# Reordering the tail of the last block: a written order for three engines, a bf16 bias product, and int8 products pulled forward

## The chip, the cores and the metric

The kernel runs on one core of a Trainium2 chip. The core has a matrix engine (TensorE, PE in the profile; its weight loads are PEld), a vector engine (VectorE, DVE), an activation engine (ScalarE, ACT), a general engine (GpSimd, POOL), and a queue engine that issues most transfers (SyncE, SP). The metric is the device time of one execution in microseconds (us); the time of a version is the median of its runs.

## What is computed

Two layers act on `x` of shape (2, 2048, 512). The first is a conditioned linear layer, a gated recurrence over the tokens and a gated MLP. The second, where the change lies, does this for every token:

```python
h = silu(cat @ int_W1 + int_b1) @ int_W2 + int_b2      # cat: six normed or shifted forms of x
y = (h - mean(h)) / sqrt(var(h) + 1e-5) * int_g + int_be
scale = max(abs(y)) / 127                              # per token
q = clip(round(y / scale), -127, 127)                  # int8 values, held as bf16
x = x + (q @ q_rhs) * scale * rhs_scale
```

## The kernel before, in words

One program does both layers. The first phase lasts to about 1392 us and works on 1024 tokens at a time. The second phase works on 8 blocks of 512 tokens (`T`), and a block is four tiles of 128 tokens (`J` = 4).

For a block, `by_tokens` and `by_channels` make the operands of the first product; `up` (its steps are those of `paired_in_place`, all products through line 134) computes the hidden values `h1` in seven steps, with half products that are reused: the steps are numbered 0 to 6, and each has a half `u` = 0 and a half `u` = 1. Helpers hang on the steps in a dictionary `then`: a key `n` runs after step n, a key `(n, u)` after that half. `added` (L1486) adds the class bias with a bf16 product against `tables[:30, 3]`. The sums are finished on VectorE (L1474, L1495, L1500), and SiLU (L1478) runs on ACT. The last half of `h1` for tokens 0 to 255 comes from `out21`, after step 6.

In blocks 0 to 6, `down2` makes the second product `h1 @ int_W2`, and the norm and the int8 part of a block are spread over the next block's steps. The last block has no next block. For it `part_norm` (from L1591) makes one tile's second product and norm, and rounds it; `part_product` (from L1613) turns the rounded values by four TensorE transposes, clamps them at -127, makes the int8 product (L1548, called from `by_rhs`), scales it (L1551), adds the residual (L1620) and stores the tile (L1621). Tiles 2 and 3 get their `part_norm` after `(6, 0)`, since their hidden values are complete then. Tiles 0 and 1 follow after step 6, and then `part_product` of tiles 2, 3, 0, 1.

In `part_norm` the bias `int_b2` is added by a product of a row of ones with the row `b2_bc[0:1]`, both f32 (L1596). An f32 product of 512 columns is two instructions on TensorE, so the four chunks of `int_W2` are eight (L1598). The norm on VectorE is: statistics from PSUM (L1320, L1321), variance plus eps (L1327), root on ACT (L1328), subtract and gain (L1533), reciprocal and a three-instruction refinement (L1329, L86 to L88), scale and shift (L1534), largest magnitude (L1537), the two scale instructions (L1045, L1046), scaling with a rounding constant added (`shifted`, L1540), and the constant taken off with the upper clamp (`rounded`, L1543).

What sets the order: each engine has a queue that it works off in order. The framework's scheduler fills the queues from simulated times and priorities (text order), so it may lift an instruction ahead of others and mix two chains. Inside `tc.manual_schedule(engines=...)` the listed engines take instructions in the order in which they are written; `ordered()` is that for PE, DVE and ACT. The first block already uses it for PE alone. Waits between engines are semaphores; SP and POOL are queues too, and a transfer that waits holds those behind it.

The second phase's small buffers come from the pool `io`, in the order in which `place` first names them: `rows` (bias, gain and shift, broadcast to 128 partitions, loaded at L1301), `int_w2`, then `pw1`, `lnT`, `tT` and so on. They lie over buffers of the first phase: in the kernel before, `pw1` begins 14,336 bytes into the pool. `split` (L1110 to L1114) cuts an f32 row into three bf16 parts whose sum is the row, on POOL, and stores the parts into `tables`; the class bias of the second phase takes this way, around 1414 us. `tables` has 128 partitions and 4 slots of 512 bf16; slot 3 uses rows 0 to 29.

Of the kernel before, what the change touches and what calls it, by code (L numbers as in the profile page):

```python
# [9 lines left out]
FP = mybir.dt.float32  # L10
BF = mybir.dt.bfloat16
AF = mybir.ActivationFunctionType
ALU = mybir.AluOpType
# [4 lines left out]
P = 128  # L18
B, L, D, F = 2, 2048, 512, 1536
C = D // P  # L20
FC = F // P
T = 512
J = T // P
# [6 lines left out]
G = 32  # L30
MAGIC = 12582912.0
# [19 lines left out]
def adaln_attn_ffn(ctx: ExitStack, tc: tile.TileContext, a: dict, out: bass.AP):  # L51
    nc = tc.nc
# [3 lines left out]
    small = ctx.enter_context(tc.tile_pool(name="small", bufs=2))  # L56
# [53 lines left out]
    def mm(name):  # L110
        return mm_ps.tile([P, T], FP, tag="mm", name=name)
# [217 lines left out]
    ones = const.tile([P, P], FP, name="ones")  # L329
# [4 lines left out]
    identb = const.tile([P, P], BF, name="identb")  # L334
# [33 lines left out]
    idle = mm("idle")  # L368
# [185 lines left out]
    def up_norm(s):  # L554
        return normed_halves(2, s, hs_d[s], "L0_attn_norm2_w")
# [297 lines left out]
    for s in range(1, NS):  # L853
        Bt, chunks = up_norm(s)
# [13 lines left out]
    rq = w3.tile([P, C, D], BF, name="rq", bufs=1)  # L868
    rsbc = w3.tile([P, D], FP, name="rsbc", bufs=1)
# [5 lines left out]
    tables = w3.tile([P, 4, D], BF, name="tables", bufs=1)  # L875
# [406 lines left out]
    def place(name, *shape, dtype=FP):  # L1282
        if name not in places:
            n = 1
            for k in shape:
                n *= k
            places[name] = io.tile([P, n], FP if dtype == FP else BF, name=name)
        t = places[name]
        if dtype != FP and t.dtype == FP:
            t = t.bitcast(dtype)  # L1290
        if len(shape) == 2:
            return t.rearrange("p (a b) -> p a b", b=shape[1])
        return t
# [8 lines left out]
    b2_bc, g_bc, be_bc = (rows[:, k, :] for k in range(3))  # L1302
    w2 = place("int_w2", C, D)
    load_w(w2, a["int_W2"])


    PAIRS = (0, 1)

    def duo(t, q):
# [4 lines left out]
    def tr(name, dtype=FP):  # L1314
        turn[0] ^= 1
        return tr_ps[turn[0]].tile([P, 2, D], dtype, tag="tr", name=name)

    def stats(mv, j, t, name):
        st = small.tile([P, 6], FP, tag="st", name=f"{name}_st_{j}", bufs=4)
        nc.vector.bn_stats(st, t)  # L1320
        held["stats"] = nc.vector.bn_aggr(mv[:, j, :], st)  # L1321

    def rstd_of(mv, name):
        n = mv.shape[1]
        r = small.tile([P, J], FP, tag="rstd", name=f"{name}_rstd", bufs=4)[:, :n]
        v = small.tile([P, 2, J], FP, tag="rv", name=f"{name}_rv", bufs=4)[:, :, :n]
        nc.vector.tensor_scalar(v[:, 0, :], mv[:, :, 1], 1e-5, None, ALU.add)  # L1327
        held["root"] = nc.scalar.activation(r, v[:, 0, :], AF.Sqrt)  # L1328
        nc.vector.reciprocal(r, r)  # L1329
        refine(r, v[:, 0, :], v[:, 1, :])  # L1330
        return r
# [36 lines left out]
    def by_tokens(i, k, behind=()):  # L1368
# [6 lines left out]
        mv = small.tile([P, J, 2], FP, tag="mv", name=f"mv1_{i}", bufs=4)  # L1375
        for q in PAIRS:
            if behind:
# [52 lines left out]
    def gains(i, k, n):  # L1430
# [4 lines left out]
        else:  # L1435

            src = block("lnT")
            dst = block("tT") if n == (not i) else src
        ps = [tr(f"gain_{i}_{n}_{q}") for q in PAIRS]
        for c in range(C):  # L1440
# [8 lines left out]
    h1s, o4s, mvs = {}, {}, {}  # L1449
# [81 lines left out]
    def gained(out_, in_, mean, r):  # L1531

        nc.vector.scalar_tensor_tensor(out_, in_, mean, g_bc, ALU.subtract, ALU.mult)  # L1533
        nc.vector.scalar_tensor_tensor(out_, out_, r, be_bc, ALU.mult, ALU.add)  # L1534

    def largest(out_, t):
        nc.vector.tensor_reduce(out_, t, AX.X, ALU.max, apply_absolute_value=True)  # L1537

    def shifted(t, inv):
        nc.vector.tensor_scalar(t, t, inv, MAGIC, ALU.mult, ALU.add)  # L1540

    def rounded(qn, t):
        nc.vector.tensor_scalar(qn, t, -MAGIC, 127.0, ALU.add, ALU.min)  # L1543

    def by_rhs(t, qT, scale, name):
        ps = m2_ps.tile([P, D], FP, tag="mm", name=name)
        for c in range(C):
            nc.tensor.matmul(  # L1548
                ps, qT[:, ts(c, P)], rq[:, c, :], start=(c == 0), stop=(c == C - 1)
            )  # L1550
        nc.vector.scalar_tensor_tensor(t, ps, scale, rsbc, ALU.mult, ALU.mult)  # L1551

    out_t = out.rearrange("(n p) d -> p n d", p=P)
# [34 lines left out]
        nc.vector.tensor_add(t, t, duo(x2n, q))  # L1588
        nc.sync.dma_start(out_t[:, i * J + 2 * q : i * J + 2 * q + 2], t)

    def part_norm(i, j):  # L1591


        h1 = h1s[i]
        ps = m2_ps.tile([P, D], FP, tag="mm", name=f"ps_o_{i}_{j}")
        nc.tensor.matmul(ps, ones[0:1, :], b2_bc[0:1, :], start=True, stop=False)  # L1596
        for c in range(C):
            nc.tensor.matmul(ps, h1[:, c, ts(j, P)], w2[:, c, :], start=False, stop=(c == C - 1))  # L1598
        mv = small.tile([P, J, 2], FP, tag="mv", name=f"mv3_{i}_{j}", bufs=4)[:, 0:1]
        stats(mv, 0, ps, f"s3_{i}_{j}")  # L1600
        r = rstd_of(mv, f"r3_{i}_{j}")
        t = place(f"o4_{j // 2}", 2, D)[:, j % 2, :]
        gained(t, ps, mv[:, 0, 0:1], r[:, 0:1])
        qs = small.tile([P, 3, J], FP, tag="qs4", name=f"qs_{i}_{j}", bufs=4)[:, :, 0:1]
        largest(qs[:, 0, :], t)
        quant_scale(qs[:, 1, :], qs[:, 2, :], qs[:, 0, :])
        shifted(t, qs[:, 2, :])

        qn = places["pw0"].bitcast(BF)[:, ts(j, D)]
        rounded(qn, t)  # L1610
        return t, qs, qn

    def part_product(i, j, t, qs, qn):  # L1613
        pt = tr(f"trq_{i}_{j}", BF)[:, 0, :]
        for c in range(C):
            nc.tensor.transpose(pt[:, ts(c, P)], qn[:, ts(c, P)], identb)
        qT = places["pw1"].bitcast(BF)[:, ts(j, D)]
        nc.vector.tensor_scalar(qT, pt, -127.0, None, ALU.max)
        by_rhs(t, qT, qs[:, 1, :], f"ps_f_{i}_{j}")
        nc.vector.tensor_add(t, t, place(f"x2n{i % 2}", J, D)[:, j, :])  # L1620
        nc.sync.dma_start(out_t[:, i * J + j], t)  # L1621

# [18 lines left out]
    for m, at in ((0, 0), (2, 2)):  # L1641
        for c in range(C):
            nc.tensor.matmul(
                pb[G * c : G * c + G], beta(m, c), w_int[at + c // 2][:, 1:4:2, c % 2, :],
                start=(m == 0), stop=(m == 2),
            )
    for c in range(C):
        nc.tensor.matmul(
            pc[G * c : G * c + G], beta(1, c), w_int[2 + c // 2][:, 0:3:2, c % 2, :],
            start=True, stop=True,  # L1650
# [40 lines left out]
    for i in range(NB):  # L1691
        nxt = load(i + 1) if i + 1 < NB else None
        then = {} if last else in_first
        if last:
            qs = []
            then[0] = lambda: qs.append(last_norm(i - 1))
            then[1] = lambda: [int8_values(i - 1, qs[0], q) for q in PAIRS]
            then[2] = lambda: int8_product(i - 1, qs[0], last["x2n"], 0, held["ins"])
            then[3, 0] = lambda: int8_product(i - 1, qs[0], last["x2n"], 1, held["ins"])
        if nxt:  # L1700
            then[3] = lambda: by_tokens(i + 1, nxt)
            then[6] = lambda: by_channels(i + 1, nxt)
        else:

            parts = {}

            def half():
                for j in (2, 3):
                    parts[j] = part_norm(i, j)
            then[6, 0] = half  # L1710
        up(i, k, then)
        if nxt:
            down2(i, nxt)
        else:
            for j in (0, 1):
                parts[j] = part_norm(i, j)
            for j in (2, 3, 0, 1):
                part_product(i, j, *parts[j])
        last, k = k, nxt


# [66 lines left out]
```

## Time and profile before

| what | value |
|---|---|
| median of 3 runs | 2020.08 us (2018.74 to 2021.53) |
| the profiled execution, its own time | 2021.65 us |
| its span | 2019.9 us |
| TensorE busy | 2001.7 us, 99% of the span |
| VectorE busy | 1174.8 us, 58% |
| ACT busy | 653.4 us, 32% |
| POOL busy | 153.8 us, 8% |

The span runs from the first to the last instruction; the execution's own time is a little longer. Busy time of an engine is the time in which it runs an instruction; a wait is not counted. "The chain that ended last" goes back from the last instruction to what released it. In the order of time, a row holds the start, the duration, the engine, the line, the operation, what is written and read, and the count of merged instructions; in square brackets stands the idle time before it and what ended it. In a row of windows, after the window and its length come the busy time and the count of PE, PEld, DVE, ACT and POOL, then the granted TensorE clock (1.00 is full), the transfer engines' busy share, and GB/s.

### The profile page before, as it was taken

The numbers are of one execution on the slowest core, as the hardware profiler recorded it, in microseconds if no ns is written. First come the engines' busy times: TensorE is split into PE (matmuls) and PEld (weight loads), VectorE is DVE, ScalarE is ACT, GpSimd is POOL, SyncE is SP. The second block draws the span as 40 slices with busy tenths as digits, with TensorE's granted clock in tenths as the row PEclk, the third lists the DMA queues.
The fourth block names the chain that finished last, engine by engine and source line by source line (L and its number), as shares of the span: only waits on it lengthen the run. The fifth ranks groups of instructions, "written<-read, shape, count | busy, mean of one in ns | idle before, by whom it ended". The sixth has DMA issues, their size and how long they took to land.

```text
span 2019.9 us, 16905 instructions
## 1 busy us (share of the span) xinstructions
PE 2001.7 (99%) x6292; PEld 1067.4 (53%) x6300; DVE 1174.8 (58%) x1783; ACT 653.4 (32%) x863; POOL 153.8 (8%) x127
## 2 busy tenths in 40 slices
PE   9999999999999999999999999989999999999998
PEld 5444444444444444444444444435877777777774
DVE  6667666666534224324325465466687687687675
ACT  4557777777522222222221000001302302302301
POOL 0141000000400000000010000061300000000000
PEclk9999999999999999999999999999999999999999
DMA  5661212121512112111335766533211211211110
GB/s 202 217 198 52 90 62 98 42 94 58 161 42 91 45 42 94 42 42 52 110 112 180 229 220 224 201 111 130 92 45 63 76 51 63 73 53 63 32 32 21
DMA packets 99332, 197.21 MB, mean 98 GB/s; under 512 B 21393, under 2 KB 49591, under 8 KB 95153
## 3 DMA queue, kind: packets, MB, share of 16 engines
q1 hardware_dynamic: 94584, 179.31, 26.4%
q0 software_dynamic: 4608, 16.78, 2.5%
q8 instruction: 50, 0.82, 0.2%
q14 instruction: 34, 0.27, 0.0%
q10 hardware_dynamic: 56, 0.03, 0.0%
HBM read 133.27 MB, written 58.75 MB: 95 GB/s over the span
## 4 chain that ended last, share of the span: by engine, by line
PE 95%; DVE 1%; issue 1%; POOL 1%; DMA 1%; ACT 0%; SPq 0%; POOLq 0%; ACTq 0%; DVEq 0%
PE up_a L134 16%; PE ps_h_a L134 11%; PE rec_a L134 11%; PE up_d L134 8%; PE dn_a L134 7%; PE ps_h_d L134 6%; PE rec_d L134 5%; PE ps_o L1524 5%; PE up_b L134 4%; PE dn_d L134 3%; PE ps_h_b L134 3%; PE y_a L134 3%; PE rec_b L134 3%; PE dn_b L134 2%; PE y_d L134 1%; PE ps_f L1548 1%
## 5 line engine op out<-in xcount | busy, mean ns | idle before, releaser
L134 PE MATMUL dn_a<-op,w_dn 128*128 128x512 f32 x384 | 169.7, 600 | 5.3 <-DVE op L222 5.3
L134 PE MATMUL up_a<-h,w_up 128*128 128x512 f32 x384 | 172.6, 592 | 0.0
L814 DVE SCALAR_TENSOR_TENSOR prod<-up_d,cols,k 128x512 f32<-128x512 f32 x48 | 36.0, 751 | 199.6 <-ACT k L297 199.6
L297 ACT COPY k<-up_a 128x512 f32<-128x512 f32 x144 | 84.0, 584 | 196.8 <-PE up_a L134 196.7
L794 ACT ACTIVATE gate<-gate,cols 128x512 f32<-128x512 f32 x96 | 68.8, 721 | 215.3 <-DVE gate L793 213.3
L134 PE MATMUL up_a<-h2T,w_up 128*128 128x512 f32 x288 | 129.5, 592 | 0.0
L134 PEld LDWEIGHTS dn_a<-op,w_dn 128*128 128x128 f32 x384 | 72.9, 192 | 95.8 <-issue 87.9
L134 PEld LDWEIGHTS up_a<-h,w_up 128*128 128x128 f32 x384 | 72.9, 190 | 91.9 <-issue 89.7
L134 PE MATMUL rec_a<-h,w_rec 128*128 128x512 f32 x256 | 115.1, 592 | 0.0
L134 PE MATMUL rec_a<-hT,w_rec 128*128 128x512 f32 x256 | 115.1, 592 | 0.0
L1524 PE MATMUL ps_o<-int_w,h 128*128 128x512 f32 x224 | 103.6, 605 | 0.0
L134 PEld LDWEIGHTS up_a<-h2T,w_up 128*128 128x128 f32 x288 | 54.7, 190 | 68.9 <-issue 68.9
L134 PE MATMUL up_b<-h,w_up 128*128 128x512 f32 x192 | 86.3, 592 | 0.0
L134 PE MATMUL up_d<-h,w_up 128*128 128x512 f32 x192 | 86.3, 592 | 0.0
L134 PE MATMUL dn_d<-op,w_dn 128*128 128x512 f32 x192 | 83.7, 594 | 0.0
L134 PEld LDWEIGHTS rec_a<-h,w_rec 128*128 128x128 f32 x256 | 48.6, 190 | 61.2 <-issue 61.2
L134 PEld LDWEIGHTS rec_a<-hT,w_rec 128*128 128x128 f32 x256 | 48.6, 190 | 61.2 <-issue 61.2
L297 ACT COPY k<-rec_a 128x512 f32<-128x512 f32 x96 | 55.7, 580 | 71.1 <-PE rec_a L134 69.5
L793 DVE TENSOR_TENSOR gate<-up_b,k 128x512 f32<-128x512 f32 x48 | 32.9, 690 | 72.2 <-PE up_b L134 71.2
L134 PE MATMUL up_d<-h2T,w_up 128*128 128x512 f32 x144 | 65.2, 592 | 0.0
L1524 PEld LDWEIGHTS ps_o<-int_w,h 128*128 128x128 f32 x224 | 40.2, 189 | 46.5 <-issue 46.5
L222 DVE TENSOR_TENSOR op<-op,op 128x3072 f32<-128x3072 f32 x16 | 55.8, 3486 | 12.3 <-PE dn_d L134 6.5
(403 smaller groups left out, 3444.4 us busy)
## 6 DMA issues: line engine op xcount, KB each, us to landing
pp_d<-prod SPq DMA_DIRECT2D x48, 512.0 KB
op<-pp_d SPq DMA_DIRECT2D x16, 1536.0 KB
y_d<-y SPq DMA_DIRECT2D x16, 512.0 KB
h<-y_d SPq DMA_DIRECT2D x4, 2048.0 KB
yr<-y_d SPq DMA_DIRECT2D x16, 512.0 KB
hs_d<-yr SPq DMA_DIRECT2D x16, 512.0 KB
h<-hs_d SPq DMA_DIRECT2D x4, 2048.0 KB
op<-in_xT SPq DMA_DIRECT2D x32, 256.0 KB
```

Source lines behind the costliest of these rows:

```text
L134: ins = nc.tensor.matmul(ps, ws[k // 2][:, slot, k % 2, ts(u, P)], xs[k], start=(first and k == 0), stop=(last and k == n - 1), skip_group ...
L222: nc.vector.tensor_sub(t, p, q)
L297: nc.scalar.copy(t, ps)
L793: nc.vector.tensor_add(gate[u][:, half], ps, kept)
L794: nc.scalar.activation(gate[u][:, half], gate[u][:, half], AF.Gelu, bias=col("L0_attn_mlp_gate_b", fs[u]),)
L814: nc.vector.scalar_tensor_tensor(prod[u][:, b_], ps, col("L0_attn_mlp_fc_b", fs[u]), kept, ALU.add, ALU.add)
L1524: nc.tensor.matmul(ps, h1[:, c, ts(j, P)], w2[:, c, :], start=(c == 0), stop=(c == C - 1))
L1548: nc.tensor.matmul(ps, qT[:, ts(c, P)], rq[:, c, :], start=(c == 0), stop=(c == C - 1))
```

## The change

Early, after `int_w2` is loaded, the row `int_b2` is cut into three bf16 rows on POOL, and SP stores these into rows 32 to 34 of slot 3 of `tables`. A bf16 tile `onesb` is filled with ones.

At the end, the class `Tile` takes the place of `part_norm` and `part_product`. The bias becomes one bf16 product of three rows of ones with the three rows. The norm's subtraction and gain are written ahead of the reciprocal. For tile 0 the rounding constant is taken off on ACT (Identity with a bias of minus the constant); the others keep `rounded`. The clamp after the transposes works on both sides. From the first half of step 6 on, PE, DVE and ACT take the written order: tiles 2 and 3 whole, tile 2's transposes and clamp, then the second half of step 6, then the order in the diff. The int8 products of tiles 2 and 3 stand ahead of tile 1's second product, and 14 products of ones with ones, whose result nobody reads, stand between tile 0's and tile 1's transposes.

```diff
+    onesb = io.tile([P, P], BF, name="onesb")
+    nc.gpsimd.memset(onesb, 1.0)
+    b2_rows, by_ones = tables[G : G + 3, 3, :], onesb[G : G + 3]
+    t = place("qT0", D)[0:1]
+    h = place("qT1", 2, D, dtype=BF)
+    nc.gpsimd.tensor_copy(t, b2_bc[0:1])
+    for n in range(3):
+        part_of = h[0:1, n % 2, :]
+        nc.gpsimd.tensor_copy(part_of, t)
+        if n < 2:
+            nc.gpsimd.tensor_sub(t, t, part_of)
+        nc.sync.dma_start(b2_rows[n : n + 1], part_of)
...
+    less_magic = small.tile([P, 1], FP, name="less_magic", bufs=1)
+    nc.vector.memset(less_magic, -MAGIC)
+    class Tile:
+        def __init__(self, i, j):
+            self.i, self.j = i, j
+            self.t = place(f"o4_{j // 2}", 2, D)[:, j % 2, :]
+            self.qn, self.qT = (places[n].bitcast(BF)[:, ts(j, D)] for n in ("pw0", "pw1"))
+        def second_product(self):
+            i, j = self.i, self.j
+            ps = self.ps = m2_ps.tile([P, D], FP, tag="mm", name=f"ps_o_{i}_{j}")
+            nc.tensor.matmul(ps, by_ones, b2_rows, start=True, stop=False)
+            self.chunks((0, 1))
+        def chunks(self, cs):
+            for c in cs:
+                nc.tensor.matmul(
+                    self.ps, h1s[self.i][:, c, ts(self.j, P)], w2[:, c, :], start=False,
+                    stop=(c == C - 1),
+                )
+        def norm(self):
...
+            nc.vector.tensor_scalar(v[:, 0, :], mv[:, :, 1], 1e-5, None, ALU.add)
+            nc.scalar.activation(r, v[:, 0, :], AF.Sqrt)
+            nc.vector.scalar_tensor_tensor(
+                t, self.ps, mv[:, 0, 0:1], g_bc, ALU.subtract, ALU.mult
+            )
+            nc.vector.reciprocal(r, r)
+            refine(r, v[:, 0, :], v[:, 1, :])
+            nc.vector.scalar_tensor_tensor(t, t, r[:, 0:1], be_bc, ALU.mult, ALU.add)
...
+            largest(qs[:, 0, :], t)
+            quant_scale(qs[:, 1, :], qs[:, 2, :], qs[:, 0, :])
+            shifted(t, qs[:, 2, :])
+            if j:
+                rounded(self.qn, t)
+            else:
+                nc.scalar.activation(self.qn, t, AF.Identity, bias=less_magic)
+        def transposed(self):
+            self.pt = tr(f"trq_{self.i}_{self.j}", BF)[:, 0, :]
+            for c in range(C):
+                nc.tensor.transpose(self.pt[:, ts(c, P)], self.qn[:, ts(c, P)], identb)
+        def clamped(self):
+            nc.vector.tensor_scalar(self.qT, self.pt, 127.0, -127.0, ALU.min, ALU.max)
...
             def half():
-                for j in (2, 3):
-                    parts[j] = part_norm(i, j)
+                end.enter_context(ordered())
+                for t in (t2, t3):
+                    t.second_product()
+                    t.chunks((2, 3))
+                    t.norm()
+                t2.transposed()
+                t2.clamped()
             then[6, 0] = half
         up(i, k, then)
...
-            for j in (0, 1):
-                parts[j] = part_norm(i, j)
-            for j in (2, 3, 0, 1):
-                part_product(i, j, *parts[j])
+            t2.last_product()
+            t0.second_product()
+            t2.scaled()
+            t2.stored()
+            t3.transposed()
+            t3.clamped()
+            t0.chunks((2, 3))
+            t3.last_product()
+            t0.norm()
+            t1.second_product()
+            t1.chunks((2, 3))
+            t0.transposed()
+            idle = m2_ps.tile([P, D], FP, tag="mm", name="idle_end")
+            for _ in range(14):
+                nc.tensor.matmul(idle[:, 0:P], ones, ones, start=True, stop=True)
+            t1.norm()
+            t1.transposed()
+            t0.clamped()
+            t3.scaled()
+            t0.last_product()
+            t1.clamped()
+            t1.last_product()
+            t3.stored()
+            t0.scaled()
+            t1.scaled()
+            t1.stored()
+            t0.stored()
+            end.close()
```

`last_product`, `scaled` and `stored` hold the same instructions as the end of `part_product`: four bf16 products, the scaling, the addition and the store.

More of the change, by code (lines that the diff above doesn't have):

```diff
@@ L1589, in int8_product @@
         nc.sync.dma_start(out_t[:, i * J + 2 * q : i * J + 2 * q + 2], t)
[L1591 to L1621, printed above, removed]
+    less_magic = small.tile([P, 1], FP, name="less_magic", bufs=1)
@@ new lines, in adaln_attn_ffn, with last_product, scaled, stored @@
+    nc.vector.memset(less_magic, -MAGIC)
[16 more added lines that the diff above has]
+        def norm(self):
+            i, j, t = self.i, self.j, self.t
+            mv = small.tile([P, J, 2], FP, tag="mv", name=f"mv3_{i}_{j}", bufs=4)[:, 0:1]
+            stats(mv, 0, self.ps, f"s3_{i}_{j}")
+            n = f"r3_{i}_{j}"
+            r = small.tile([P, J], FP, tag="rstd", name=f"{n}_rstd", bufs=4)[:, 0:1]
+            v = small.tile([P, 2, J], FP, tag="rv", name=f"{n}_rv", bufs=4)[:, :, 0:1]
+            nc.vector.tensor_scalar(v[:, 0, :], mv[:, :, 1], 1e-5, None, ALU.add)
[6 more added lines that the diff above has]
+            nc.vector.scalar_tensor_tensor(t, t, r[:, 0:1], be_bc, ALU.mult, ALU.add)
+            qs = self.qs = small.tile([P, 3, J], FP, tag="qs4", name=f"qs_{i}_{j}", bufs=4)[:, :, 0:1]
+            largest(qs[:, 0, :], t)
[11 more added lines that the diff above has]
+            nc.vector.tensor_scalar(self.qT, self.pt, 127.0, -127.0, ALU.min, ALU.max)
+        def last_product(self):
+            ps = self.ps = m2_ps.tile([P, D], FP, tag="mm", name=f"ps_f_{self.i}_{self.j}")
+            for c in range(C):
+                nc.tensor.matmul(
+                    ps, self.qT[:, ts(c, P)], rq[:, c, :], start=(c == 0), stop=(c == C - 1)
+                )
+        def scaled(self):
+            nc.vector.scalar_tensor_tensor(
+                self.t, self.ps, self.qs[:, 1, :], rsbc, ALU.mult, ALU.mult
+            )
+        def stored(self):
+            i, j = self.i, self.j
+            nc.vector.tensor_add(self.t, self.t, place(f"x2n{i % 2}", J, D)[:, j, :])
+            nc.sync.dma_start(out_t[:, i * J + j], self.t)
@@ L1703, in adaln_attn_ffn @@
         else:
-            parts = {}
+            end = ExitStack()
+            t0, t1, t2, t3 = (Tile(i, j) for j in range(J))
             def half():
-                for j in (2, 3):
-                    parts[j] = part_norm(i, j)
+                end.enter_context(ordered())
[5 more added lines that the diff above has]
+                t2.clamped()
             then[6, 0] = half
```

## The prediction

> **What bounds the kernel now.** I read the page first, then the chain that ended last from 1960 us on, then the order of time on each engine from 1978 us, then the last 20 us cut into windows.
>
> ```profile
> span 2019.9 us, 16905 instructions
> PE 2001.7 (99%) x6292; PEld 1067.4 (53%) x6300; DVE 1174.8 (58%) x1783; ACT 653.4 (32%) x863; POOL 153.8 (8%) x127
> PE   9999999999999999999999999989999999999998
> ```
>
> TensorE is never free for long: up to the last block all that is not on TensorE is hidden. The change touches two places only, the start of the second phase (about 1400 us) and the end. The chain shows where the end leaves TensorE:
>
> ```profile
> 1985.70 1.05 PE ps_o L1596 x2
> 1986.75 3.63 PE ps_o L1598 x8
> ...
> 1999.69 3.65 PE ps_o L1598 x8
> 2003.34 0.02 issue
> 2003.36 0.70 DVE s_st L1320
> ...
> 2013.28 1.90 PE ps_f L1548 x4
> 2015.18 0.03 issue
> 2015.21 0.76 DVE zone_A L1551
> 2015.97 0.02 issue
> 2015.99 0.69 DVE zone_A L1620
> ```
>
> TensorE bounds until 2003.34, then VectorE, except two TensorE pieces near the end. The last addition ends at 2016.68, and its store closes the span 3.22 later. In VectorE's own order its first norm starts at 1985.73, so 30.95 us lie between. Of these VectorE is idle 0.76 + 2.31 + 0.76 + 1.39 = 5.2. So the end is VectorE work (25.7) with few holes, not a TensorE queue alone.
>
> **The new end, step by step.** Unit prices, start to start, from rows like these (start, duration):
>
> ```profile
> 1998.68 0.70 DVE L1320 BATCH_NORM_STATS2 s_st<-ps_o 128x6 f32<-128x512 f32 x1 [2.31 <-PE ps_o L1598]
> 2001.92 0.69 DVE L1537 TENSOR_REDUCE qs<-zone_A 128x1 f32<-128x512 f32 x1
> 2010.05 0.68 DVE L1537 TENSOR_REDUCE qs<-zone_A 128x1 f32<-128x512 f32 x1
> 2011.67 0.43 DVE L1543 TENSOR_SCALAR zone_B<-zone_A 128x512 bf16<-128x512 f32 x1
> 2012.15 0.34 PEld L1616 LDWEIGHTS <-zone_B 128*128 128x128 bf16 x4 [1.12 <-DVE zone_B L1543]
> ```
>
> One norm, stats to reduce, is 3.24; reduce to rounding 1.62; the rounding reaches TensorE 0.49 later: 5.35. An independent VectorE instruction can start 0.34 after the rounding's start, so a norm holds VectorE 5.20. Run strictly one after the other, norms lose the overlap of two chains that the free order has now. Clamp (L1618) holds 0.35 and reaches TensorE after 0.47; scaling (L1551) holds 0.66, or 0.78 before its own addition; addition (L1620) 0.62.
>
> The bias: now two f32 passes of one row, 1.05 (L1596). The new bf16 product of three rows is in no row. Below it lies 0.22 (a 512-column bf16 product at full clock: the x3 group at 1959.83 takes 0.81), above it the present 1.05. I take 0.30, nearest to the bf16 row, with 0.1 for the weight load. Saved per tile 0.75; but tile 2's bias now lies in a hole at 1970 where TensorE waits for ACT anyway, so it saves nothing.
>
> That hole, and one at 1978.6 that holds the first chunk of tile 2 (1.12), can't be filled any more if the written order is kept strictly, since tile 2's products then stand behind the first half of the last step. That half starts at 1979.27 in place of 1979.51 (its weight load at 1979.08 waits for VectorE L1474 both times) and ends at 1982.7. From there:
>
> Tile 2: bias 0.30, chunks 3.54, pipeline 0.1: stats at 1986.65, now 1985.73. Norm: TensorE sees it at 1992.0, VectorE turns to tile 3 at 1991.85. TensorE ends tile 3 at 1990.4 and then stands before tile 2's transposes, which are queued ahead of the last half step. This is a new wait of 1.6, and everything on TensorE is behind it: transposes 0.4, half step 3.45, class rows 0.32, to 1996.2. Tile 3's norm holds VectorE to 1997.05, tile 2's clamp reaches TensorE at 1997.5: a second wait, 1.3. The int8 product (4 x 0.24, from 7 in 1.67 at 2004.73) ends at 1998.5. VectorE is idle 1.1 meanwhile, then scales and stores tile 2 until 2000.0. TensorE does tile 0's bias and two chunks (2.07), tile 3's transposes (0.35): clamp at 2000.95, idle 1.0 before. Chunks 2 and 3 of tile 0 end at 2002.65; their SiLU on ACT (table 1.28, 0.84, from 1996.2) was done at 1998.4. VectorE idle 1.3, stats of tile 0 at 2002.7.
>
> Tile 0's rounding goes to ACT. The nearest row is the Identity at L601, 0.78 with no table load before it after a Sqrt (20.19 us). So VectorE is free at 2002.7 + 4.77 = 2007.5, TensorE gets tile 0 at 2008.4. Meanwhile it did tile 3's product (to 2003.6) and all of tile 1 (3.84, to 2007.45). Tile 1's stats: 2007.55. Its root on ACT comes 1.1 later, behind that Identity, done at 2008.4: no wait; a table change would cost 1.3 to 2.
>
> Fourteen idle products follow. At the program's start 18 instructions of this form (nine calls) take 4.05 start to start [...]: 0.225 each, so 0.11 at full clock and 28 x 0.11 = 3.2, to 2012. Tile 1 reaches TensorE at 2012.9: they fit. If weight loads bound them (0.19 as beside the f32 products) they take 5.3 and delay the end by 1.3.
>
> The tail on VectorE from 2012.75: clamp 0 (0.35), scale 3 (0.66), clamp 1 at 2013.75, add 3 (0.62), scale 0 at 2014.75, scale 1 at 2015.4, add 1 at 2016.2, add 0 at 2016.8, end 2017.5. TensorE's two last products run 2013.3 to 2015.2, just in time at full clock. The store adds 3.22; tile 1's store goes out 0.6 before it, and one store's data takes 0.75, so at most 0.2 more. End: **2020.7, which is 0.8 over 2019.9**. Counted the other way: VectorE's work by these steps is 27.4 without overlap, against 25.7; its holes fall from 5.2 to 3.4; it starts 0.9 later: 1.7 - 1.8 + 0.9 = 0.8.
>
> **The clock, a rule against the row.** The windows show it granted 1.00 to 2010.0 and then:
>
> ```profile
> 2010.50:2011.00 0.50, 0.50 (x3) 0.22 (x2) 0.43 (x3) 0.00 (x0) 0.00 (x0) 0.50 0.45 176
> ```
>
> Now TensorE is idle 2006.8 to 2010.2 and the last two products take 1.75 and 1.89. [...] By my waits (1.6 at most) [...] the products take 0.95 each. If the gaps were enough to drop the clock, both take 0.9 more and the end is 2022.6. The trace's 2004 to 2010, busy under half and still granted 1.00, speaks for full clock.
>
> **The constants at 1400 us.** POOL gets a memset, four casts or copies and two subtractions, SP three small stores into rows 32 to 34 of the tables. Nearest rows:
>
> ```profile
> 1414.54 1.64 POOL L1110 CAST q<-bias 10x512 bf16<-10x512 f32 x1 [27.05 <-ACT bias L1667]
> 1416.26 2.01 POOL L1112 TENSOR_TENSOR bias<-bias,q 10x512 f32<-10x512 f32 x1
> 1416.20 6.24 SPq L1114 DMA_DIRECT2D tables<-q  x3
> ```
>
> They need `rows`, issued by SP at 1399.56, landed by about 1402 (estimate from the store's 2 to 3 us). Sum 0.9 + 1.64 + 2.01 + 1.49 + 1.14 + 0.60 = 7.8, so POOL is free at 1410, 4.5 before the class sums, and SP is free before it must store the class tables. SP's load of the next block (1401.43) may stand behind these three waits, to 1410; with 5 us it lands 10 us before TensorE's 1424.89. The three new tiles stand ahead of `pw1` in their pool, so `pw1` moves onto the last `dk` buffers: its gathers (1385.31) may wait about 1.2 for stores issued until 1384.5; they are used at 1396.55, with 3 to spare. All hidden: 0.
>
> Against this: [...] while POOL casts, the L222 sums take 1.63 and 2.17, not 1.22. Between 1402 and 1410 VectorE has four normalisations (0.5) and small sums that TensorE nearly waits for. By the row, half of 0.5 more on each would be up to 1; by no rule 0. I take 0.1.
>
> **Sum.** 0.8 + 0.1 = 0.9. The profiled execution took 2021.65 (span 2019.9 and 1.75 around it), so 2022.5 by it; it lies 1.6 above the median of the runs. On the median: 2020.08 + 0.9 = **2021.0**.
>
> **Rivals.**
> 1. The scheduler still lifts tile 2's first products into the two holes (0.20). For it: the order holds only within its section, and it does so now. Against: the products come after a half step that is written first. Stats stay at 1985.73, all is 0.9 earlier: 2020.1.
> 2. VectorE runs without holes (0.10). Started at 1985.7 as in rival 1, its 27.4 end at 2013.1 and the span at 2016.3: 3.6 less, 2016.5 on the median; half a microsecond of steps that I took too dear carries it past 4. Against: the three holes are waits written into the order.
> 3. Slower, late class tables (0.14). TensorE needs the third table at 1424.36, some 2 after its store, so there is hardly slack. If POOL's new work starts behind 1406.6 in place of 1402 (late rows, or the queue puts it there), every microsecond passes to TensorE; from about 1410 it costs over 4. Starting at 1412 gives 2026.
> 4. The half clock or slow idle products: 2022.4 to 2023 (0.10, of which 0.02 reaches past 4).
>
> The rest, 0.46, is the likeliest, 2019.5 to 2022.5 by itself. What a measurement can tell is 0.2%, 4.0 us. Case 2 gives faster 0.10; case 3 and the tail of 4 slower 0.16; the rest 0.74. The range leaves out the half of case 2 and of case 3: 2017.2 to 2024.8.
>
> **What would show it.** Stats of tile 2 near 1986.6 (1985.7: rival 1); TensorE idle about 1.6 and 1.3 around the last half step; three VectorE holes near 1 each; clock 1.00 to the last product, 0.95 each; the last addition near 2017.5; TensorE without a new wait at 1424. A TensorE gap there, or VectorE without holes, makes it wrong.

## The result and the profile after

The changed kernel takes 2022.07 us (median of 22 runs, 2018.28 to 2025.39), the kernel before in the same comparison 2019.28 us (22 runs). The ratio is 1.0015, 95% interval 1.0009 to 1.0021: slower by 1.8 to 4.2 us, 3.0 in the middle. The interval leaves out 1, so the loss is real. Its middle is below the 0.2% that the prediction set as its bound, so it counts as the same, and the time lies inside the range. The forecast was +0.9.

The profiled execution hides this. Its own time is 2020.94 and its span is 0.8 shorter than that of before. The head of the page after:

```profile
span 2019.1 us, 16970 instructions
PE 1998.4 (99%) x6315; PEld 1068.3 (53%) x6324; DVE 1178.0 (58%) x1783; ACT 654.1 (32%) x864; POOL 159.5 (8%) x134
PE   9999999999999999999999999989999999999997
```

TensorE still bounds all but the end. To compare the two places that the change touches, I cut each trace at instructions that both kernels have. A runs from the start of the span to the first transpose of `tr_oh`, on TensorE at about 1392 us, just before the second phase; up to there the two kernels have the same TensorE work. B runs from there to the first product of `ps_h_d` in block 0, and holds the new constants. C follows up to the bias product of tile 2 in the last block. D runs from that product to the end of the last addition, and E to the end of the span.

| us | A | B | C | D | E |
|---|---|---|---|---|---|
| before | 1392.40 | 24.96 | 552.71 | 46.61 | 3.22 |
| after | 1390.56 | 26.46 | 552.75 | 46.25 | 3.08 |

C is unchanged. The end (D and E) gained 0.50. The start (B) lost 1.50. A was 1.84 shorter. A scatters by up to 4 us between the traces of all these kernels (1388.44 to 1392.58), and a second trace of the changed kernel has 1392.38, so the shorter span is luck and not the change.

**The end.** TensorE in the order of time after, with start and duration, and the idle time in brackets:

```profile
1969.77 0.38 PE L1621 MATMUL ps_o<-tables,onesb 3*128 3x512 bf16 x1
1977.99 1.12 PE L1626 MATMUL ps_o<-int_w,h 128*128 128x512 f32 x2
1990.53 0.40 PE L1658 MATMUL trq<-identb,zone_B 128*128 128x128 bf16 x4 [1.44 <-DVE zone_B L1557]
1996.06 1.04 PE L1666 MATMUL ps_f<-rq,pw 128*128 128x512 bf16 x3 [1.30 <-DVE pw L1661]
2007.23 3.34 PE L1793 MATMUL idle_end<-ones 128*128 128x128 f32 x28
2011.52 0.40 PE L1658 MATMUL trq<-identb,zone_B 128*128 128x128 bf16 x4 [0.94 <-DVE zone_B L1557]
2012.08 1.80 PE L1666 MATMUL ps_f<-rq,pw 128*128 128x512 bf16 x7 [0.16 <-issue]
```

The first two rows are tile 2's bias and its first chunk. They still lie in the holes at 1970 and 1978, ahead of the first half of step 6, though they are written behind it. The next two waits are the new ones that the prediction named. The last row is the end of the int8 products at full speed, and a window over it shows the clock:

```profile
2012.00:2014.00 2.00, 1.80 (x7) 0.51 (x6) 2.00 (x5) 0.00 (x0) 0.00 (x0) 1.00 0.00 0
```

The chain that ended last after the change, with start and duration of its pieces, now stays on VectorE from tile 2's statistics on, but for 5.3 us of TensorE between 1996.06 and 2001.36:

```profile
1979.98 2.59 PE ps_h_a L134 x12
1982.57 2.59 PE ps_o L1626 x6
1985.18 0.71 DVE s_st L1334
...
1995.67 0.34 DVE pw L1661
...
1999.55 1.79 PE ps_o L1626 x4
2001.36 0.71 DVE s_st L1334
...
2014.73 0.69 DVE zone_A L1677
```

**The start.** POOL in the order of time after:

```profile
1387.48 0.94 POOL L1377 DMA_INDIRECT pw<-in_pw,idx_pw  x1 [4.31 <-DMA x<-dk]
...
1399.13 0.60 POOL L1312 COPY qT<-rows 1x512 f32<-1x512 f32 x1 [8.50 <-DMA rows<-in_rows]
...
1402.38 1.15 POOL L1317 TENSOR_TENSOR qT<-qT,qT 1x512 f32<-1x512 f32 x1
1405.25 0.60 POOL L1315 CAST qT<-qT 1x512 bf16<-1x512 f32 x1 [1.72 <-DMA tables<-qT]
```

Before, the first gather into `pw1` waited for no store:

```profile
1385.31 0.94 POOL L1363 DMA_INDIRECT pw<-in_pw,idx_pw  x1 [0.30 <-issue]
```

Now (1387.48) it waits 4.31 for the store of the last `dk` buffer, and the next gather and the memset of `onesb` stand behind it on POOL's queue, to 1388.72 and 1390.39. The casts of the row begin at 1399.13 and run into what VectorE does next:

```profile
1394.95 1.23 DVE L1422 TENSOR_TENSOR pw<-zone_C,pw 128x1024 f32<-128x1024 f32 x1 [1.51 <-DMA pw<-in_pw,idx_pw]
...
1400.01 0.41 DVE L1341 TENSOR_SCALAR r_rv<-mv 128x4 f32<-128x4 f32 x1
...
1401.86 0.46 DVE L87 TENSOR_TENSOR r_rv<-r_rv,r_rstd 128x4 f32<-128x4 f32 x1
...
1402.55 1.72 DVE L1348 TENSOR_SCALAR zone_B<-zone_B,mv,r_rstd 128x512 f32<-128x512 f32 x2
```

Before, the two small operations (L1341 and L87 here) took 0.16 each and the two normalisations of the last row 1.00:

```profile
1403.20 0.16 DVE L87 TENSOR_TENSOR r_rv<-r_rv,r_rstd 128x4 f32<-128x4 f32 x1
...
1403.60 1.00 DVE L1334 TENSOR_SCALAR zone_B<-zone_B,mv,r_rstd 128x512 f32<-128x512 f32 x2
```

Together that is 1.27 more (0.25, 0.30 and 0.72), on a chain on which TensorE stands: at its next transposes (`tr_h`) it waits 0.74 for `lnT` from VectorE, where before it did not wait. Before, then after:

```profile
1406.82 1.04 PE L1343 MATMUL tr_h<-ident,zone_B 128*128 128x128 f32 x8
1406.38 1.09 PE L1357 MATMUL tr_h<-ident,zone_B 128*128 128x128 f32 x8 [0.74 <-DVE lnT L1461]
```

The new stores don't explain this: the first slowed operation starts at 1400.01, while POOL works, and SP issues the first store only at 1400.42; from 1404.20, with POOL idle, two normalisations take 0.99 again.

### The profile page after: what moved, and what is told of

The parts are those of the page before. It is cut to its first block, busy times and chain, and to the rows that moved or that the text cites. A ratio compares the mean times of both kernels' runs of the same rounds, so it can differ in the third digit from the quotient of the medians.

```text
span 2019.1 us, 16970 instructions
## 1 busy us (share of the span) xinstructions
PE 1998.4 (99%) x6315; PEld 1068.3 (53%) x6324; DVE 1178.0 (58%) x1783; ACT 654.1 (32%) x864; POOL 159.5 (8%) x134
## 4 chain that ended last, share of the span: by engine, by line
PE 95%; DVE 3%; DMA 1%; issue 1%; POOL 0%; ACT 0%; SPq 0%; DVEq 0%; POOLq 0%; ACTq 0%
PE up_a L134 16%; PE rec_a L134 11%; PE ps_h_a L134 11%; PE up_d L134 8%; PE dn_a L134 8%; PE ps_h_d L134 6%; PE rec_d L134 5%; PE ps_o L1538 5%; PE up_b L134 4%; PE dn_d L134 3%; PE y_a L134 3%; PE ps_h_b L134 3%; PE rec_b L134 3%; PE dn_b L134 2%; PE y_d L134 1%; PE ps_f L1562 1%
## 5 line engine op out<-in xcount | busy, mean ns | idle before, releaser
L222 DVE TENSOR_TENSOR op<-op,op 128x3072 f32<-128x3072 f32 x16 | 55.7, 3484 | 12.9 <-PE dn_d L134 7.1
```

The source lines that it names most:

```text
L222: nc.vector.tensor_sub(t, p, q)
```

## The experiments

The theory from here on: the end is a small gain and the start a larger loss. The loss comes from POOL's casts, which slow VectorE, and from the later gathers. The rivals: the order of the end loses time that one trace doesn't show; or the longer time is a scatter of the start that has nothing to do with the constants. The expectations that speak of 40.5 to 42.0 for the start count it from an earlier instruction, from where it measured 40.51 before and 42.00 after; the text below uses B.

**The changed kernel once more** (no edit).

> The changed kernel once more, for a second trace. Stretches, by TensorE's starts: A, from the program's start to the first of the last 36 dn_a products (1376.85 before, 1375.02 changed); B, from there to the first ps_h_d product of block 0 (40.51 before, 42.00 changed); C, from there to the bias product of tile 2 (552.71 and 552.75); D, from there to the end of the last addition (46.61 and 46.25). Theory 1 (the start of the second phase pays): B again 1.5 over the kernel before, D 0.3 to 0.4 under it, A scatters by 2 either way without a cause in the change; the time 1 to 3 us over the kernel before. Theory 2 (the end pays in most executions and this trace was a lucky one): D over 46.6 this time.

2022.48 us, ratio 1.0015 (1.0007 to 1.0024). D is 46.25 again, to 0.01. B is 28.89, now 3.93 over the 24.96 of before. So the end repeats, and the loss lies in the start, where its size differs between executions.

**The constants without the shifted buffers.** `pw1` keeps its old place, the casts stay:

```
+    place("pw1", 2, 2 * D)
     onesb = io.tile([P, P], BF, name="onesb")
```

> The changed kernel with one line more: pw1 is named ahead of the three new tiles, so it keeps its place in the pool and its gathers wait for no dk store. The POOL casts stay where they are. Theory 1a (the shifted buffer is the cost: gathers later by 4 us, and what follows): B falls back to 40.5 to 40.8 and the time to 0.5 under the kernel before. Theory 1b (POOL's casts slow VectorE's instructions, 0.25 + 0.30 + 0.72 in the changed trace): B stays at 41.7 to 42.0, the gathers follow each other as before, and the time stays 1 to 3 us over the kernel before. Theory 2: no change in B's share, time as the changed kernel.

> The changed kernel with pw1 in its old place once more, so the casts without the shift. Theory 1b: B 25.3 to 26.2 (25.57 in the first trace) with a wait of TensorE at the transposes of zone_B, D 46.25, time 0 to 1.5 us over the kernel before. If the first trace was scatter: B 24.1 to 25.0, no wait there.

The gathers follow one another without waiting for a store (1383.25 and 1384.49 in the first trace). B is still 25.57 and 28.06 in the two traces, and the ratios are 1.0009 (1.0001 to 1.0018) and 1.0017 (1.0010 to 1.0024). The casts alone make most of the loss. The second trace shows how it gets so large. VectorE in the order of time there:

```profile
1402.98 2.20 DVE L1349 TENSOR_SCALAR zone_B<-zone_B,mv,r_rstd 128x512 f32<-128x512 f32 x2
1405.10 1.83 DVE L1349 TENSOR_SCALAR pw<-pw,mv,r_rstd 128x512 f32<-128x512 f32 x2
```

All four normalisations take 4.03 where they took 2.00. TensorE, in the order of time of the same trace:

```profile
1408.12 1.20 PE L1358 MATMUL tr_h<-ident,zone_B 128*128 128x128 f32 x8 [2.20 <-DVE lnT L1462]
1409.25 1.97 PE L1358 MATMUL tr_h<-ident,pw 128*128 128x128 f32 x8
```

It waits 2.20, and the next eight transposes take 1.97 where the first kernel's took 1.09. The windows of that trace (the granted clock is the first of the last three numbers):

```profile
1408.00:1409.00 1.00, 0.88 (x8) 0.86 (x8) 1.00 (x2) 0.00 (x0) 0.00 (x0) 0.99 1.03 434
1409.00:1410.00 1.00, 1.00 (x6) 0.75 (x5) 0.97 (x3) 0.65 (x1) 0.00 (x0) 0.50 0.81 337
...
1412.00:1413.00 1.00, 1.00 (x6) 0.83 (x5) 0.00 (x0) 0.27 (x1) 0.00 (x0) 0.80 0.00 0
```

From 1409.0 to 1412.4 by these windows, for 3.4 us, the clock is half. From the start of `tr_h` to the instruction behind the eight products that follow, TensorE then needs 5.40 in place of 3.77. The second trace of the changed kernel shows the same: a wait of 2.17, then 5.29. After waits of 0.74, 1.21 and 1.39 the clock stayed full (10.64 to 10.66 behind `tr_h` in the table below, 12.06 and 12.16 with the half clock).

**The shifted buffers without the constants.** The kernel before, with three buffers of the same size that nobody uses:

```
+    shift = io.tile([P, P], BF, name="shift")
+    nc.gpsimd.memset(shift, 1.0)
+    place("qT0", D)
+    place("qT1", 2, D, dtype=BF)
```

> The kernel before with three tiles of the same sizes named ahead of pw1 and one POOL memset, and none of the casts and stores: the shift by 4,352 bytes alone. B is now counted from the start of the one-hot transposes (tr_oh, 1392.40 before) to the first ps_h_d product: 24.96 before, 26.46 and 28.89 in two traces of the changed kernel, 25.57 with pw1 in its old place, 26.96 with the new start alone, 24.71 with the casts made later. Theory 1a (the shift makes the gathers of pw wait 4 us for the dk stores): B 25.8 to 28, time 1 to 2.5 us over the kernel before. Theory 1b (the casts slow VectorE): B 24.7 to 25.0, time as before.

> The shift by 4,352 bytes alone once more, since its trace and its time did not agree (B 26.25, 1.3 over the kernel before; time 1.0001 with an interval of 0.0008 to both sides). Theory 1a: B 25.8 to 28 again, time 0.5 to 2.5 us over the kernel before. If it is hidden: B 24.1 to 25.0 and the time as before.

The gather waits 4.31 and 4.41, VectorE stands 2.55 and 1.76 for it, and B is 26.25 and 25.46: 1.29 and 0.50 more. VectorE's row of the first trace:

```profile
1396.34 1.23 DVE L1413 TENSOR_TENSOR pw<-zone_C,pw 128x1024 f32<-128x1024 f32 x1 [2.55 <-DMA pw<-in_pw,idx_pw]
```

The ratios, 1.0001 (0.9993 to 1.0009) and 1.0008 (1.0000 to 1.0016), hardly resolve that. In the two traces of the changed kernel this wait of VectorE was only 1.51 and 0.91, and TensorE's class sums behind it were 0.24 and 0.08 later than before. So the shift is the smaller part there.

**The start alone.** The kernel before with all of the new start (the first hunk of the change), whose rows nobody reads:

> The kernel before with the change's new code at the start of the second phase alone (tiles, casts, three stores); nothing reads the bias rows, and the end is that of the kernel before. Theory 1: B 42.0, D 46.6, time 1.5 to 3 us over the kernel before. Theory 2: the time of the kernel before within 0.5 us.

1.0011 (1.0004 to 1.0017), 2.2 us slower. D is 46.61 as before, B 26.96. The start makes the kernel slower without the end.

**The constants later.** The changed kernel, with the casts behind a gather of block 1 (POOL at about 1425), and with its buffers named last in the pool:

```
-    onesb = io.tile([P, P], BF, name="onesb")
...
+    def bias_rows(behind):
+        onesb.append(io.tile([P, P], BF, name="onesb"))
...
+        with tc.issue_after(behind.ins):
...
+                then[3] = steps(then[3], lambda: bias_rows(held["gather"]))
```

> The changed kernel with the bias rows made on POOL behind block 1's gathers (about 1427 us), with the new tile last in the pool: neither the shift nor the casts lie in stretch B. Theory 1 (either form): B back to 40.5, D 0.3 to 0.4 under the kernel before, time 0.2 to 0.6 us under the kernel before. Theory 2: the time stays 2 to 3 us over the kernel before, D over 46.6.

B is 24.71 and D 46.26, with no wait at `tr_h`. In the order of time of VectorE the normalisations are back at 1.00:

```profile
1400.79 1.00 DVE L1352 TENSOR_SCALAR zone_B<-zone_B,mv,r_rstd 128x512 f32<-128x512 f32 x2
```

The time, 1.0003 (0.9994 to 1.0011), can't tell the 0.6 us of gain that the stretches show from nothing; its middle is a loss of 0.6. C is 552.74, so the casts cost nothing at their new place either. What follows is that the loss has gone from the start.

Where the casts fell decides how large the loss is. Here is each trace; the second column is how long before the first normalisation POOL's work began, and its first five instructions last 4.4 to 4.6 us:

| trace | ahead | four normalisations | `tr_h` later | behind `tr_h` | B |
|---|---|---|---|---|---|
| before | none | 2.00 | 0 | 10.54 | 24.96 |
| late constants | none | 2.00 | -0.24 | 10.53 | 24.71 |
| after | 3.42 | 2.71 | 1.40 | 10.64 | 26.46 |
| start alone | 3.24 | 2.90 | 1.88 | 10.66 | 26.96 |
| old place of `pw1` | -0.48 | 3.49 | 0.50 | 10.65 | 25.57 |
| the same, second | 1.35 | 4.03 | 1.48 | 12.16 | 28.06 |
| after, second | 0.85 | 4.13 | 2.41 | 12.06 | 28.89 |

"Later" is the start of `tr_h` counted from `tr_oh`, past the 14.42 of before. With the old place of `pw1`, VectorE reaches this work 0.9 earlier after `tr_oh` than before, which covers part of its loss. Casts that begin about a microsecond ahead cover all four normalisations, and these then take twice their time. In both such traces the clock was halved too, and that cost 1.5 and 1.6 more. Why the casts begin at another moment each time is open. They wait for `rows`, whose load was issued 5.2 us after `tr_oh` in the first trace of the changed kernel and 7.4 in the second. In the kernels without casts at this place it scatters as much (7.2 before, 5.3 in the second trace of the shifted buffers), so the casts don't cause the shift; what does was not separated.

**When a wait halves the clock.** The length of one wait does not decide. The kernel before and the one with the start alone have the same wait of 3.39 ahead of tile 0's int8 product. TensorE in the order of time, before:

```profile
2010.19 1.75 PE L1548 MATMUL ps_f<-rq,pw 128*128 128x512 bf16 x4 [3.39 <-DVE pw L1618]
```

With the start alone:

```profile
2008.49 1.04 PE L1563 MATMUL ps_f<-rq,pw 128*128 128x512 bf16 x4 [3.39 <-DVE pw L1633]
2010.45 0.61 PE L1631 MATMUL trq<-identb,zone_B 128*128 128x128 bf16 x4 [0.93 <-DVE zone_B L1558]
2011.58 1.89 PE L1563 MATMUL ps_f<-rq,pw 128*128 128x512 bf16 x4 [0.52 <-DVE pw L1633]
```

Before, the four products right behind the wait took 1.75: the clock was 1.00 to 2010 and 0.50 from 2010.5 on. With the start alone the four right behind it took 1.04, as at full clock (1.03 at 2001.16 after the change, granted 1.00), and only the next four took 1.89, with 0.50 from 2012 to 2014. At the start of the second phase, waits of 2.17 and 2.20 were enough. What decides behind which of these waits the clock falls was not shown, so that it fell in both may be chance.

**Without the idle products.** The loop of 14 and its tile are left out; the rest is the changed kernel.

> The changed kernel without the fourteen products whose result nobody reads. Theory (they hold the clock): TensorE is then idle for some 4 us ahead of tile 1's transposes, the granted clock falls to 0.5, tile 0's and tile 1's int8 products take 1.75 each in place of 0.95, and D (bias product of tile 2 to the end of the last addition) grows from 46.25 to 47.3 to 48.1. Rival (the clock would hold without them, they are idle work): D stays 46.2 to 46.3. B as in the changed kernel.

TensorE in the order of time, tile 1's transposes and the last two int8 products, and a window over them with the clock at 0.50:

```profile
2010.57 0.61 PE L1658 MATMUL trq<-identb,zone_B 128*128 128x128 bf16 x4 [4.12 <-DVE zone_B L1557]
2010.97 3.62 PE L1666 MATMUL ps_f<-rq,pw 128*128 128x512 bf16 x8
...
2010.00:2012.00 2.00, 1.44 (x7) 0.85 (x8) 1.97 (x6) 0.00 (x0) 0.00 (x0) 0.50 0.00 0
```

Eight products take 3.62, where after the change the seven in the trace took 1.80. D is 47.89, 1.64 more, and the ratio is 1.0020 (1.0014 to 1.0027). The idle products are worth 1.6 us.

**The f32 bias in the new order.** The start is left out with it:

```
-            nc.tensor.matmul(ps, by_ones, b2_rows, start=True, stop=False)
+            nc.tensor.matmul(ps, ones[0:1, :], b2_bc[0:1, :], start=True, stop=False)
```

> The changed kernel's written order with the bias as in the kernel before (a row of ones with the f32 row) and nothing at the start of the second phase. Theory (the bf16 bias is what pays for the waits of the written order): the biases of tiles 0 and 1 lie on the way to VectorE and cost 0.75 each, so D is 47.5 to 47.9 in place of 46.25; B 24.7 to 25.0. Time 0.5 to 1.2 us over the kernel before. Rival (the bias lies beside VectorE's work): D 46.2 to 46.6, time 0.3 under the kernel before.

D is 47.98, 1.73 more than with bf16 rows, B 24.12. The written order with the old bias loses 1.37 at the end against the kernel before. So the bias pays, and the order by itself costs. The ratio is 1.0004 (0.9997 to 1.0010).

**Another order, first form.** Late constants, and an order meant to fill VectorE's holes: tile 3's norm behind the last half step with tile 2's clamp inside it, tile 0's clamp inside tile 1's norm, ten idle products:

```
-                    t.norm()
-                t2.transposed()
-                t2.clamped()
+                t2.norm()
...
+            t2.transposed()
+            t3.norm(t2.clamped)
```

> The kernel with late bias rows and another written order: the second half of step 6 ahead of tile 2's transposes, tile 2's clamp within tile 3's norm and tile 0's within tile 1's, tile 2's int8 product between tile 0's halves, and the finished tiles' scalings and additions while TensorE makes the last product; ten idle products. Theory (the holes that the written order makes on VectorE, 1.13 + 0.98 + 1.35, are what the end could still give): D 42.6 to 43.6, so the time is 2.5 to 4 us under the kernel before. Rival (other waits take their place): D over 45.

D is 49.00, a clear miss: 2.4 worse than before. ACT in the order of time:

```profile
1991.07 1.28 ACT L1496 ACT_TABLE_LOAD   x1 [6.42 <-PE ps_h_a L1504]
1992.36 0.84 ACT L1496 ACTIVATE h<-ps_h_a,cols 128x256 f32<-128x256 f32 x2
1993.22 1.28 ACT L1643 ACT_TABLE_LOAD   x1
1994.51 0.20 ACT L1643 ACTIVATE r_rstd<-r_rv 128x1 f32<-128x1 f32 x1
```

VectorE in the order of time of the same trace:

```profile
1994.75 0.17 DVE L1647 RECIPROCAL r_rstd<-r_rstd 128x1 f32<-128x1 f32 x1 [4.49 <-ACT r_rstd L1643]
```

Written behind the half step, tile 3's root stands on ACT's queue behind the SiLU of that half step, with a table load ahead of each, and VectorE waits 4.49 for it. I had followed the order on VectorE and TensorE and not on ACT. The ratio is 1.0010 (1.0003 to 1.0016).

**Another order, second form.** Late constants and ten idle products here too. Both norms of tiles 2 and 3 stand ahead of the second half of step 6 again. Tile 2's transposes and clamp come behind it, so TensorE needn't wait for the rounding; tile 0's chunks are ahead of the int8 products, and tile 2 is scaled and stored only after tile 1's norm:

```
                     t.norm()
-                t2.transposed()
-                t2.clamped()
...
-            t2.last_product()
+            t2.transposed()
+            t2.clamped()
             t0.second_product()
-            t2.scaled()
-            t2.stored()
-            t3.transposed()
-            t3.clamped()
             t0.chunks((2, 3))
-            t3.last_product()
+            t2.last_product()
+            t3.transposed()
             t0.norm()
...
+            t3.clamped()
+            t3.last_product()
...
-            t1.norm()
+            t1.norm(t0.clamped)
+            t0.last_product()
...
+            t2.scaled()
+            t2.stored()
```

The third form has tile 2's int8 product ahead of tile 0's last two chunks, and scales and stores tile 2 before tile 0's norm.

> As less_waits, mended where its trace showed the new wait: tile 3's norm is again written ahead of the last half of step 6, so that its root does not stand behind SiLU in ACT's queue (4.49 us of VectorE idle). Tile 2's clamp follows tile 3's norm, tile 0's second half product goes ahead of tile 2's int8 product, tile 2's scaling and addition wait until tile 1's norm is done. Theory (holes on VectorE make D): one hole of about 1.3 before tile 0's norm, D 43.1 to 43.9 (46.25 changed, 46.61 before); time 2.5 to 4 us under the kernel before. Rival (VectorE's holes only move): D over 45.5.

> As less_waits_2, but tile 2's int8 product ahead of the second half of tile 0's product, so that VectorE scales and stores tile 2 while it would wait: work in the hole, in return a wait of TensorE for the clamp. Theory: about 0.3 worse than less_waits_2, D 43.4 to 44.2; time 2 to 4 us under the kernel before. Rival: D over 45.5.

D is 43.81 and 43.88. From tile 2's statistics on VectorE has one hole left, of 1.18 in the second form and of 1.13, with a rest of 0.24, in the third. Its order of time in the second form:

```profile
1981.29 0.70 DVE L1338 BATCH_NORM_STATS2 s_st<-ps_o 128x6 f32<-128x512 f32 x1 [5.92 <-PE ps_o L1630]
...
1993.29 0.70 DVE L1338 BATCH_NORM_STATS2 s_st<-ps_o 128x6 f32<-128x512 f32 x1 [1.18 <-PE ps_o L1630]
...
2009.00 0.69 DVE L1683 TENSOR_TENSOR zone_A<-zone_A,x2n 128x512 f32<-128x512 f32 x1
```

The ratios are 0.9985 (0.9979 to 0.9992) and 0.9987 (0.9979 to 0.9995). The second form, 2016.66 us against 2019.12, is about 3 us faster than before by the ratio: less than the 0.2% bound, but clear of noise. It beats both kernels.

**The sums agree.** The changes of B and D against before, added, beside the time by the ratio (times 2019):

| kernel | B + D, from traces | time |
|---|---|---|
| after | +1.1 and +3.6 | +3.0 (1.8 to 4.2) |
| start alone | +2.0 | +2.2 (0.8 to 3.4) |
| old place of `pw1` | +0.3 and +2.7 | +1.8, +3.4 |
| shifted buffers | +1.3 and +0.5 | +0.2, +1.6 |
| late constants | -0.6 | +0.6 (-1.2 to 2.2) |
| no idle products | +2.7 | +4.0 (2.8 to 5.5) |
| f32 bias | +0.5 | +0.8 (-0.6 to 2.0) |
| other order, first | +2.2 | +2.0 (0.6 to 3.2) |
| other order, second | -3.0 | -3.0 (-4.2 to -1.6) |
| other order, third | -2.7 | -2.6 (-4.2 to -1.0) |

In the six kernels with neither casts nor shifted buffers at this place, B lies between 24.1 and 25.0, so about 0.5 of each entry is scatter.

Every kernel with the new end also holds a new constant of 4 bytes per partition (`less_magic`). That was not tried by itself; the f32 bias has it without the rest of the start, and its B (24.12) shows no loss.

## Why the prediction was right or wrong

**The forecast** of no change above 0.2% was right, with the time in the range. The +0.9 was 2 us too low. Two of its terms were wrong, with opposite signs: the end gained where a loss of 0.8 was forecast, and the constants cost many times the 0.1 allowed. That they partly cancel is luck.

**"That hole, and one at 1978.6 ... can't be filled any more" failed.** The prediction held that the written order starts at a fixed place and keeps tile 2's bias and first chunk behind the half step. The scheduler still lifted both ahead of it (rows at 1969.77 and 1977.99): rival 1, given 0.20. Counted from the start of that half step, tile 2's statistics begin 6.23 later (before 6.22), where the step had 7.38. That takes 1.15 off its +0.8 and leaves a gain of 0.35 to the last addition. Measured is 0.36, and 0.14 more at the store. (The quarter microsecond that the shorter bias sets free ahead of the half step was in the prediction.)

**From the statistics on, the steps held.** Statistics to last addition: 30.85 predicted, 30.84 measured. TensorE's waits: 1.6 and 1.3 predicted, 1.44 and 1.30 measured. VectorE's three holes: 1.1, 1.0 and 1.3 predicted, 1.13, 0.98 and 1.35 measured:

```profile
1997.13 0.75 DVE L1671 SCALAR_TENSOR_TENSOR zone_C<-ps_f,qs,rsbc 128x512 f32<-128x512 f32 x1 [1.13 <-PE ps_f L1666]
1999.59 0.42 DVE L1661 TENSOR_SCALAR pw<-trq 128x512 bf16<-128x512 bf16 x1 [0.98 <-PE trq L1658]
2001.36 0.70 DVE L1334 BATCH_NORM_STATS2 s_st<-ps_o 128x6 f32<-128x512 f32 x1 [1.35 <-PE ps_o L1626]
```

The three-row bias takes 0.32 in the chain (0.30 taken). The rounding on ACT takes 0.72 with no table load (0.78). The 28 idle instructions take 3.34 (3.2) and fit: 0.12 each at a granted 1.00, where 0.11 was an estimate from 0.225 at the program's start. The clock stays 1.00. So rival 4 did not happen, and rival 2 was excluded by the three holes; the other orders show that it was within reach, since they end 2.4 us earlier with fewer holes.

**The constants, "I take 0.1", is the mis-sized term.** It measured 1.5 in one trace and 3.9 in the other. Three steps were off:
- "Half of 0.5 more on each would be up to 1": where POOL works all the while, each normalisation takes 1.0 in place of 0.5 (four in 4.03 and 4.13), which is the full 0.5 each, 2 in all, and the small operations around the root and the refinement take up to 0.5 more each (0.63 in place of 0.16 with the start alone). The trace of before already had a row with nearly that ratio, the L222 sums at 2.17 in place of 1.22 beside POOL's work: it spoke against "all hidden", and I took a tenth of its price. The sums with an operand in PSUM (L1461) kept their length beside POOL: 1.21 at 1400.33, where 1.22 was taken before.
- The clock was weighed at the end only. Here the wait for the slowed VectorE reached 2.17 and 2.20, and the clock was half for 3.4 us behind it. That added 1.5. At the end the full clock came out right: from 2004 to 2016 it is 1.00, and TensorE's waits there are 0.94 at most. But the time from 2004 to 2010, busy under half and granted 1.00, did not speak for it: in the same trace the clock was 0.50 from 2010.5 on, behind the wait of 3.39.
- "May wait about 1.2": the gathers waited 4.3, because the store of `dk`, issued at 1382.31, let them go only at 1387.48. With 3 to spare the wait reached VectorE as 0.9 to 1.5. It moved TensorE by 0.1 to 0.2 in the changed kernel, and by 0.5 and 1.3 in the shift alone.

**Rival 3** (late class tables) did not happen: POOL was free at 1405.85 or 1409.4, and TensorE reads the third table without a wait in both traces (1424.0, 1428.3). Its place was right, its mechanism not: the price of POOL's work came through VectorE and not through POOL's queue.

## What to carry to other kernels

Work on POOL isn't hidden because POOL is idle: look at what VectorE does in the same microseconds, and whether TensorE stands behind it: the same seven instructions cost 0.6 to 3 us at 1400 us and nothing measurable at 1425. A new buffer named early in a pool shifts all later ones onto other dying buffers, so look up whose store each shifted buffer waits for. When you write an order by hand, follow it on every queue that it binds (a root written behind a half step waited 4.5 us on ACT), and check in the trace where the written order really starts. A wait of about 2 us can cost TensorE its clock: behind 2.17 and 2.20 it was half for 3.4 us here, while behind one of 3.39 the next four products took 1.04 in one trace and 1.75 in another. So look up the granted clock behind each long wait.

## What was not expected of the hardware

A normalisation on VectorE (128x512, f32) takes about twice as long while POOL works on a single row of 512: four in 4.13 in place of 2.00. A wait of TensorE of 2.2 us was enough for 3.4 us of half clock behind it, while behind one of 3.39 the next four products took 1.75 in one trace and 1.04, full clock, in another. The store of `dk` released its waiter 5 us after its issue, where I had reckoned with 2 to 3.
